# A masked graph layer on one core: PSUM banks redistributed, order constants moved to VectorE, the planned order replaced

## The chip, the cores and the metric

The kernel runs on one core of one Trainium2 chip. The metric is the device time of one execution in microseconds, from several executions of the same program; the median is used. A profile is one further execution, recorded by the hardware profiler. Its span (first to last instruction) is a little shorter than the device time of the same execution.

## The reference

`x` is 4096 x 64, `adj` is 4096 x 4096 (float32, about 67 MB), `weight` is 64 x 64.

```
h = relu(layernorm(x))                        # over the 64 features
support = h @ weight
mask = (adj != 0)
rank = cumsum(mask, axis=1); deg = rank[:, -1:]
k = min(deg, 100)
pos = rank - (deg - k)
w = mask * where(pos > 0, 0.5 ** (k - pos), 0)
out = x + w @ support + bias
```

So each set element of a row of `adj` gets the weight 0.5 to the power of the number of set elements behind it in the row, except that only the last 100 of a row count. The 67 MB of `adj` have to come into the core once; nothing else is large.

## The kernel before, in words

Rows of `adj` are taken in 32 tiles of 128 rows. Two tiles make one unit `u`, two units one group `g` (512 rows), whose sums lie in one PSUM bank. Within a row, the 4096 columns are eight blocks `h` of 512.

The pipeline of one tile `t`, each step one function:

- `load` (L295, on the queue of SyncE): 2 MB from memory into one of four buffers `a_sb` (`NA = 4`). Tiles 0, 1, 28, 29, 30 and 31 are loaded as two halves of 1 MB (`STEP`). The load of tile t needs the buffer of tile t-4, so it waits for that tile's `convert`.
- `convert` (L496, VectorE): float32 to one byte, 64 or 65. One instruction for each load, so of 4096 elements per partition or, where the load is a half, of 2048.
- `flip` (L506, VectorE): 32 x 32 transposes, so that columns of `adj` lie along partitions.
- `totals` (L512, TensorE): counts of set elements by block of 32, into a PSUM bank of pool `t`.
- `split` (L517, ScalarE): reads these counts as bytes into SBUF.
- `suffix` (L526, TensorE): counts behind each block, into a bank of pool `t`.
- `clamp` (L530, VectorE): caps them.
- `place` (L538 and L542, TensorE): the exponent of each element, into four banks of pool `v`, one for each `j`.
- `weigh` (L551, ScalarE): the exponential, four instructions of 1024 elements per partition, each frees one bank of `v`. Tile 31 has three parts of each (`PARTLY`, `PARTED`), 12 instructions.
- `aggregate` (L559, TensorE): weights times `support`; 32 matmuls for each unit, issued in eight pieces of four.

After the last unit of a group come `drain` (L572, ScalarE, adds the bias), `turn_back` (L580, TensorE, transposes), `finish` (L586, VectorE, adds `x`) and, after several groups, `store` (L590, the queue of SyncE). The last group is drained in two pieces (drains 7 and 8, for units 14 and 15).

Ahead of the tiles stands a setup: `fetch` loads `x` (L298), `turn`/`turned` transpose it, `center`, `square`, `relu`, `spread`, `root`, `power`, `support`, `scale` make the layer norm and the product with `weight`, and `first`/`second` split the result `hr` in two halves of its precision (L479 ScalarE, L482 VectorE). Its intermediate data lie in one of the two buffers of weights (`early`, `NW = 2`), so the `weigh` of tile 2, which needs that buffer, waits for all four `second`. Constants for the counting are made on GpSimd: `constants(1)` (L400 to L414, for `place`) and `order_of` (L375 to L389, for `suffix` and `count`).

PSUM has one bank for `t` (`NB = 1`), six for `v` (`NV = 6`) and one for the groups' sums. A buffer of pool `t` takes a whole bank, and totals and suffix of all tiles, and `turn_back`, share the one.

The order of the instructions on every engine is fixed when the program is built. `plan()` holds a list of tasks with a duration, a lag, needs, and a due time from the table `DUE`, plays them forward, and emits them in the order in which they start. `add_manual_dep` at the end keeps each engine in this order. So a change of a number in `DUE` moves instructions, and an engine waits at whatever instruction the order puts next. `warm` fills planned gaps of TensorE with matmuls of zeros (L423).

Of the kernel before, what the change touches and what calls it, by code (L numbers as in the profile page):

```python
# [23 lines left out]
EPS = 1e-5  # L24
# [7 lines left out]
STEP = {t: 4 for t in (0, 1, 28, 29, 30, 31)}  # L32
LOADS = [(t, h, h + STEP.get(t, 8)) for t in TILES for h in range(0, 8, STEP.get(t, 8))]

PARTLY = {31}
PARTED = (0, 1, 0, 2), (1, 2, 0, 1), (1, 2, 1, 2)
DRAINS = [(g, 0, 4, True) for g in range(7)] + [(7, 0, 2, True), (7, 2, 4, True)]
STORES = [(0, 0, 16), (1, 0, 12), (1, 12, 14), (1, 14, 16)]
NA, NM, NT, NW, NV, NB = 4, 4, 4, 2, 6, 1

DUE = {
    "fetch": [-1003, -1847],
    "load": [65, 1148, 1192, 1344, 890, 882, 1059, 807, 177, 1469, 585, 426, -306, 496, -49, 266, 921, 615, 495, 273,
    509, 817, 887, 432, 1250, 832, 1156, 645, 31, 863, 872, 512, 638, 869, 1362, 792, 926, 1009],
    "load_rest": [-481],
    "turn": [-213, 892, -361, 828, -409, -147, 168, -107],
    "turned": [-404, -273, 1152, 128, 503, 511, 433, -263],
    "center": [-857, -641, -1350, -827],
    "square": [139, -1681, -2148, -2029],
    "relu": [217, 890, -64, 143],  # L50
    "spread": [-1274, -1134, -743, -201],
    "support": [458, 166, -823, -732],
    "scale": [31, 1087, -17, 582],
    "root": [-38],
    "power": [-305],
    "constants": [-1199, 288],
    "order_of": [1110],
    "count": [174],
    "counted": [-242],
    "first": [1030, 859, 446, 134],  # L60
    "second": [869, 310, 488, 149],
    "convert": [799, 235, 213, 621, 871, 221, 1137, 339, 665, 170, 840, 839, 269, 846, 1322, 763, 1208, 992, 1053, 1092,
    755, 1566, 506, 1283, 1017, 914, 1881, 1297, 1713, 1456, 1930, 1878, 1817, 1254, 2527, 1603, 1404, 1849],
    "flip": [755, -234, 295, -127, 442, -299, 314, 236, -95, 42, 943, 437, 1189, 848, 1722, 445, 670, 663, 1043, 1071,
    1018, 1159, 1502, 907, 1558, 1730, 1512, 1723, 625, 1907, 1701, 1739, 1719, 1519, 1418, 1515, 1365, 795],
    "totals": [163, 587, 208, 187, -888, 339, 133, -152, 475, 1157, 159, 135, 674, 545, 1071, 817, 439, 1024, 1281,
    1461, 443, 2052, 963, 1181, 926, 1932, 1537, 584, 1513, 1671, 1316, 1615],
    "split": [-294, -174, -1849, -575, -454, -698, -618, -971, -742, -275, 300, 6, -214, 155, -90, -143, 509, 616, 114,
    395, 584, 524, 615, 13, 506, 320, 818, 391, 1992, 1302, 1105, 460],
    "suffix": [265, 470, 626, 553, 76, 351, -120, 701, -560, 193, 222, 311, 159, 444, 810, -221, 772, 1294, 1743, 886,  # L70
    718, 429, 591, 1159, 1296, 2185, 1511, 1501, 2001, 1496, 2127, 1546],
    "clamp": [-739, 475, 354, 317, -585, 294, 102, -276, 538, 118, 920, -398, 130, 1157, 352, 866, 900, 81, -363, 492,
    698, 1569, 702, 757, 515, 1132, 736, 1149, 1495, 1590, 1729, 1541],
    "place": [841, 96, 498, 879, 824, 837, 808, 522, 1103, 1914, 1312, 1548, 862, 1225, 743, 1302, 1785, 1644, 1994,
    1697, 1566, 1560, 1577, 1633, 2537, 1922, 1847, 2364, 2393, 2364, 1714, 1845],
    "weigh": [1655, 1181, 868, 631, 1236, 404, 1584, 1443, 897, 269, 877, 841, 328, 1501, 418, 1096, 1670, 1095, 1290,
    1045, 1295, 1247, 1314, 999, 672, 1559, 1035, 1631, 1070, 1779, 1431, 1276, 2029, 1311, 1734, 1852, 1556, 1640,
    1599, 1881, 1168, 1820, 1423, 545, 1375, 1271, 1659, 2299, 2395, 2281, 2155, 2139, 2062, 2491, 1666, 1651, 1902,
    1875, 1618, 2485, 1751, 1754, 2523, 1796, 2184, 2358, 1409, 2593, 2132, 1541, 1713, 2047, 1583, 1456, 1562, 2282,
    1641, 1846, 1727, 2021, 2924, 2344, 2590, 1925, 1978, 2498, 1946, 1761, 2622, 1817, 2190, 1884, 1953, 2032, 2057,  # L80
    2381, 2020, 2701, 1854, 2394, 2313, 2255, 1976, 2259, 1957, 2012, 1591, 2429, 2382, 2260, 2365, 3172, 2928, 2044,
    3150, 1958, 2643, 2675, 2150, 3338, 2587, 2729, 2343, 2953, 1990, 2517, 2778, 3358, 2745, 2645, 3479, 2076, 3183,
    2758, 2299, 2866],
    "aggregate": [254, 1326, 1623, 59, 522, 1349, 93, 1245, 247, 484, 1268, 1686, 2132, 1190, 2358, 448, 974, 1308,
    1356, 611, 856, 1518, 486, 1545, 1236, 918, 398, 1827, 1513, 1406, 1117, 1500, 1296, 1193, 452, 1811, 1260, 1164,
# [4 lines left out]
    2628, 2119, 2143, 2488, 2511, 1602, 2160, 1962, 2594, 2032, 2291, 2585, 1920, 2821],  # L90
    "drain": [82, 374, 29, 620, 400, 1392, 1843, 1544, 1599],
    "turn_back": [572, 1129, 645, 1544, 2558, 1512, 1987, 1280, 2435],
    "finish": [79, 927, -547, 514, 1225, 592, 1061, 2342, 2532],
    "store": [8458, 8834, 7981, 9977],
}
WAIT = 250, 60, 150, 60, 0
PE, DVE, ACT, POOL, SP = range(5)


def tasks():  # L100
# [534 lines left out]
```

## Time and profile before

| | |
|---|---|
| median of 3 runs | 188.83 us (188.54 to 188.94) |
| the profiled execution: its own time, its span | 188.37 us, 186.7 us |
| TensorE matmul busy (modelled) | 164.9 us, 88% of the span |
| ScalarE busy | 152.1 us, 82% |
| VectorE busy | 146.8 us, 79% |
| GpSimd busy | 18.9 us, 10% |
| moved by DMA | 69.55 MB, mean 373 GB/s over the span |
| `weigh` L551, 136 instructions | 123.2 us, mean 1028 ns |
| `convert` L496, 38 instructions | 84.8 us, mean 2238 ns |
| `aggregate` L559, 512 matmuls | 74.6 us, mean 291 ns |
| `flip` L506, 38 instructions | 40.7 us, mean 1072 ns |
| `split` L517, 32 instructions | 20.3 us, mean 634 ns |
| `clamp` L530, 32 instructions | 15.4 us, mean 481 ns |

The page cuts the span into 40 equal slices of 4.67 us. A digit is the busy share of a slice in tenths. Busy times of single instructions overlap somewhat when they follow each other closely, so four `weigh` of 1081 ns take some 3.7 us, not 4.3. In a timeline each line is a start, a length, an engine, a source line, an operation, its output and input, and how many instructions were merged; in brackets stands the idle time before it and what ended it.

### The profile page before, as it was taken

What the parts mean: (1) busy time and instruction counts of PE and PEld (TensorE: products, weight loads), DVE (VectorE), ACT (ScalarE), POOL (GpSimd) and SP (SyncE); (2) the same over time, 40 slices, a digit from 0 to 9 for tenths busy, and PEclk for the clock granted to TensorE, in tenths of its full rate; (3) what the DMA queues carried; (4) which work ended last, traced back from release to release, by engine and by line L of the source; (5) the groups of instructions that cost most, each with busy time, mean ns of one, the idle gap of its engine ahead of it and who ended that gap; (6) DMA issues with size and microseconds to landing.
All of it is one profiled execution on the core that took longest, in us unless ns stands there. A gap on an engine that the chain in (4) does not pass through costs nothing.

```text
span 186.7 us, 4747 instructions
## 1 busy us (share of the span) xinstructions
PE 164.9 (88%) x2080; PEld 127.3 (68%) x2080; DVE 146.8 (79%) x152; ACT 152.1 (82%) x198; POOL 18.9 (10%) x57
## 2 busy tenths in 40 slices
PE   7999699647989899889998997999898979897982
PEld 5957367435857768667676775877775858685881
DVE  3187499999999997799797899879798989993100
ACT  2773176912999999699999999999969799999951
POOL 7899500000000000000000000000000000000000
PEclk9997569999999999999999999999999999999999
DMA  6999999999999999999999999999999999940020
GB/s 202 390 427 435 435 420 425 416 428 428 428 414 428 434 414 432 428 414 442 411 428 428 418 432 421 418 446 411 428 421 414 413 420 416 417 201 0 12 90 16
DMA packets 6597, 69.55 MB, mean 373 GB/s; under 512 B 944, under 2 KB 1200, under 8 KB 1712
## 3 DMA queue, kind: packets, MB, share of 16 engines
q1 hardware_dynamic: 6416, 69.21, 88.4%
q8 instruction: 16, 0.26, 0.6%
q10 hardware_dynamic: 160, 0.03, 0.1%
q14 instruction: 5, 0.04, 0.1%
HBM read 68.19 MB, written 1.05 MB: 371 GB/s over the span
## 4 chain that ended last, share of the span: by engine, by line
ACT 36%; PE 32%; DVE 15%; POOL 10%; issue 5%; POOLq 0%; ACTq 0%
ACT wk L551 29%; PE acc L559 19%; DVE m L496 7%; ACT sums L517 5%; PE ps L526 5%; PE po L580 3%; DVE mt L506 3%; PE v L542 2%; DVE behind L530 2%; PE v L538 2%; PE tot L512 2%; ACT acc_sb L572 1%; DVE wk L472 1%; DVE hr L482 1%; POOL where L414 1%
## 5 line engine op out<-in xcount | busy, mean ns | idle before, releaser
L551 ACT ACTIVATE wk<-v 128x1024 fp32r<-128x1024 uint8 (+2 forms) x136 | 123.2, 1028 | 2.3 <-PE v L542 2.1
L496 DVE TENSOR_SCALAR m<-a_sb 128x4096 uint8<-128x4096 f32 (+1 forms) x38 | 84.8, 2238 | 5.0 <-DMA a_sb<-in_adj_dram 5.0
L559 PE MATMUL acc<-wk,hr 128*128 128x256 f32 x512 | 74.6, 291 | 3.7 <-ACT wk L551 2.2
L559 PEld LDWEIGHTS acc<-wk,hr 128*128 128x128 f32 x512 | 64.0, 188 | 10.6 <-ACT wk L551 4.3
L506 DVE STREAM_TRANSPOSE mt<-m 128x1024 f32<-128x1024 f32 (+1 forms) x38 | 40.7, 1072 | 0.4
L517 ACT ACTIVATE sums<-tot 128x512 f16<-128x512 uint8 x32 | 20.3, 634 | 16.4 <-PE tot L512 16.4
L530 DVE TENSOR_SCALAR behind<-ps,excess 128x256 f16<-128x256 f32 x32 | 15.4, 481 | 14.1 <-PE ps L526 13.9
L526 PEld LDWEIGHTS <-far 128*128 128x128 f16 x224 | 17.9, 101 | 1.9 <-POOL far L389 1.0
L526 PE MATMUL ps<-sums,far 128*128 128x224 f16 (+6 forms) x224 | 18.5, 225 | 0.7 <-POOL far L389 0.7
L512 PE MATMUL tot<-mt,band 128*32 128x256 f16 x256 | 13.5, 288 | 5.3 <-DVE mt L506 4.3
L538 PE MATMUL v<-behind,where 32*128 32x256 f16 x256 | 13.6, 276 | 2.7 <-DVE behind L530 2.3
L542 PE MATMUL v<-mt,tri 32*32 32x512 f16 x512 | 14.5, 401 | 0.0
L586 DVE TENSOR_TENSOR xr<-po,xr 128x256 f32<-128x256 f32 (+1 forms) x9 | 3.5, 393 | 12.4 <-PE po L580 12.3
L423 PE MATMUL none<-junk 128*128 128x256 bf16 x74 | 11.9, 318 | 1.1 <-DVE junk L307 1.1
L512 PEld LDWEIGHTS <-band 128*32 128x32 f16 x256 | 4.1, 95 | 11.3 <-DVE mt L506 6.1
L423 PEld LDWEIGHTS <-junk 128*128 128x128 bf16 x87 | 8.8, 109 | 3.8 <-DVE junk L307 1.1
L526 PE MATMUL ps<-sums,near 128*128 128x256 f16 x32 | 9.2, 286 | 2.0 <-ACT sums L517 1.8
L572 ACT ACTIVATE acc_sb<-acc,bias_sb 128x512 f32<-128x512 f32 (+1 forms) x9 | 6.1, 679 | 5.4 <-PE acc L559 5.4
L580 PE MATMUL po<-both,acc_sb 128*128 128x64 f32 x64 | 8.7, 275 | 1.9 <-DVE behind L530 1.3
L580 PEld LDWEIGHTS po<-both,acc_sb 128*128 128x128 f32 x64 | 7.8, 191 | 2.8 <-DVE behind L530 1.5
L538 PEld LDWEIGHTS <-where 32*128 32x128 f16 x256 | 4.5, 92 | 7.5 <-issue 4.7
L542 PEld LDWEIGHTS <-tri 32*32 32x32 f16 x512 | 4.4, 88 | 6.9 <-issue 6.9
(86 smaller groups left out, 91.0 us busy)
## 6 DMA issues: line engine op xcount, KB each, us to landing
a_sb<-in_adj_dram SPq DMA_DIRECT2D x26, 2048.0 KB, 15.3
a_sb<-in_adj_dram SPq DMA_DIRECT2D x12, 1024.0 KB, 13.2
xr<-in_x_dram SPq DMA_DIRECT2D x2, 512.0 KB, 3.9
out_dram<-xr SPq DMA_DIRECT2D x1, 512.0 KB, 17.1
out_dram<-xr SPq DMA_DIRECT2D x1, 384.0 KB, 2.3
out_dram<-xr SPq DMA_DIRECT2D x2, 64.0 KB, 1.6
w<-in_L_gnn_weight_dram ACTq DMA_DIRECT2D x2, 16.0 KB, 5.8
bias_sb<-in_L_gnn_bias_dram SPq DMA_DIRECT2D x1, 0.2 KB, 18.8
```

The source lines that it names most:

```text
L423: nc.tensor.matmul(idle[0][:, idle[1]:idle[1] + 2 * P], junk[:, :P], junk, start=not accs, stop=not accs, skip_group_check=True)
L496: nc.vector.tensor_scalar(words[n][:, :(k1 - k0) * P, :].rearrange("p (h q) e -> p h e q", q=P), tiles[t][:, k0 * W:k1 * W].rearrange("p ( ...
L506: nc.vector.transpose(to[:, k0:k1], m_v.rearrange("p (h c l) -> p h c l", c=4, l=SUB))
L512: nc.tensor.matmul(tot[SUB * c:SUB * (c + 1), :V], band[:, SUB - 12 - 4 * a:2 * SUB - 12 - 4 * a], masks[t][:, c, :, a], start=(a == 0), s ...
L517: nc.scalar.activation(sums8[t], pts.pop((t, "n"))[:, :V].bitcast(U8).rearrange("p (i f) -> p f i", f=4)[:, :2, :], AF.Copy, bias=-136.0)
L526: nc.tensor.matmul(o, l, m, start=(k == 0), stop=(k == len(todo) - 1), skip_group_check=True)
L530: nc.vector.tensor_scalar(behind[t], pts.pop((t, "s"))[:, :V], excess, float(MAX_NEIGH), op0=ALU.subtract, op1=ALU.min)
L538: nc.tensor.matmul(vs[t, j][:, a, :], where[q, a, :], behind[t][q, :], start=(a == 0), stop=False, skip_group_check=True)
L542: nc.tensor.matmul(vs[t, j][SUB * c:SUB * (c + 1), :, :], tri[q, q], masks[t][q, c, :, :].rearrange("p i a -> p a i"), start=False, stop=T ...
L551: nc.scalar.activation(wts[u][:, s0:s1, 8 * a0:8 * a1, i, j, :], v[:, s0:s1, 8 * a0:8 * a1], AF.Exp, scale=-LN2, bias=-38.0 * LN2)
L559: nc.tensor.matmul(accs[g][:, at:at + 2 * P], hr[:, h * 4 + 2 * a + s, :, :].rearrange("p s d -> p (s d)"), wts[u][:, s, 8 * a + h].rearra ...
L580: nc.tensor.matmul(pts["o", d][:, k, :], sums[d][:, k * P:(k + 1) * P], both, start=True, stop=True)
```

## The change

- PSUM: pool `t` gets two banks (`NB = 2`), pool `v` five (`NV = 5`).
- `order_of` runs on VectorE instead of GpSimd, ahead of the first tile; `stack` (the constants made from the identity) comes after it. `constants(1)` on GpSimd works on 8 and 32 columns and is broadcast in its last step. The squares get a buffer of their own, so that they no longer share that of the scaled support.
- Tiles 28, 29 and 30 are loaded whole; 0, 1 and 31 in halves (`HALF_LOADS`). Every `convert` is of half a tile, 64 instructions in all. Both halves of a tile that is loaded whole wait for its one load.
- Tile 31 has two parts by column block instead of three, 8 `weigh` instructions; `aggregate` takes its pieces of four matmuls by column block `h` instead of by slot and half.
- Code for units of half a tile (`HALF_UNITS`) and for weights made by VectorE (`QUICK`: `encode`, `take`) is added, with both sets empty: all weights are made by ScalarE, as before.
- The tables `DUE` and `FREE`, and with them the order on all engines. At the end, as built: VectorE has, from tile 30 on, convert 30 twice, clamp 29, flip 30, convert 31 twice, clamp 30, flip 31 twice, finish 6, clamp 31. TensorE has place 30, turn_back 6, totals 31, 12 matmuls of aggregate 14, suffix 31, 8 of aggregate 14, place 31, 12 of aggregate 14, 4 of aggregate 15, turn_back 7, 28 of aggregate 15, turn_back 8. In the kernel before, VectorE has convert 30, flip 30, convert 30, clamp 29, flip 30, convert 31, flip 31, convert 31, clamp 30, flip 31, clamp 31, finish 6, and TensorE has turn_back 6 after place 31, the rest in the same places. ScalarE's order at the end is the same in both, but for the parts of tile 31.

```diff
-STEP = {t: 4 for t in (0, 1, 28, 29, 30, 31)}
-LOADS = [(t, h, h + STEP.get(t, 8)) for t in TILES for h in range(0, 8, STEP.get(t, 8))]
-
-PARTLY = {31}
-PARTED = (0, 1, 0, 2), (1, 2, 0, 1), (1, 2, 1, 2)
+HALF_LOADS = {0, 1, 31}
+HALF_UNITS = set()
...
+LOADS = pieces(HALF_LOADS)
+PIECES = pieces(HALF_LOADS | HALF_UNITS)
+UNITS = pieces(HALF_UNITS)
+
+PARTS = {31: ((0, 4), (4, 8))}
+QUICK = set()
...
-NA, NM, NT, NW, NV, NB = 4, 4, 4, 2, 6, 1
+NA, NM, NT, NW, NV, NB = 4, 4, 4, 2, 5, 2
...
-FREE = 4250, 4450, 5000, 4600, 700
+FREE = 4250, 1300, 3000, 4700, 700
...
-    xt = early[:, 2 * B * D:3 * B * D]
     xs = early[:, :B * D].rearrange("p (b d) -> p b d", d=D)
-    rx = early[:, B * D:2 * B * D].rearrange("p (b i) -> p b i", i=P)
+    xt, sq, rx = (early[:, i * B * D:(i + 1) * B * D] for i in (1, 2, 3))
...
     def order_of():
-        vec = nc.gpsimd
+        vec = nc.vector
...
-            pick, more = (setup.tile([P, 2, P], F32, name=n) for n in ("pick", "more"))
-            idx_v = idx.rearrange("p a j l -> p a (j l)")
+            pick, more = (setup.tile([P, 8], F32, name=n) for n in ("pick", "more"))
+            idx_v = idx.rearrange("p a j -> p (a j)")
...
+    def stack():
+        nc.vector.tensor_add(both, ident[:, :D], ident[:, D:])
+        for h in range(H):
+            q = slice(h * D, (h + 1) * D)
+            nc.vector.tensor_scalar(less[q, h, :], ident[q, q], -1.0 / D, None, op0=ALU.add)
...
+    def half():
+        return ps_t.tile([P, V], F32, tag="t", name="sums")
...
+    def convert(n, i):
+        t, h0, _ = PIECES[n]
+        if i == 0:
+            words[n] = bpool.tile([P, N // E, E], U8, name="m8")
+        h = h0 + 4 * i
+        nc.vector.tensor_scalar(words[n][:, 4 * i * P:4 * (i + 1) * P, :].rearrange("p (h q) e -> p h e q", q=P),
+                                tiles[t][:, h * W:(h + 4) * W].rearrange("p (h e q) -> p h e q", e=E, q=P),
                                 0.0, 64.0, op0=ALU.not_equal, op1=ALU.add)
...
+    def weights(n, part):
+        t, h0, h1 = UNITS[n]
         u, i = t // 2, t % 2
         if u not in wts:
             wts[u] = wpool.tile([P, 2, 16, 2, 4, SUB], F32R, name="wk")
-        a0, a1, s0, s1 = PARTED[part] if t in PARTLY else (0, 2, 0, 2)
-        v = vs[t, j].rearrange("p a i -> p (a i)").bitcast(U8).rearrange("p (x r f) -> p f x r", f=4, r=SUB)
-        nc.scalar.activation(wts[u][:, s0:s1, 8 * a0:8 * a1, i, j, :], v[:, s0:s1, 8 * a0:8 * a1], AF.Exp, scale=-LN2, bias=-38.0 * LN2)
-
-    def aggregate(u, k):
+        x = slice(*(2 * h for h in PARTS.get(n, ((h0, h1),))[part]))
+        return wts[u][:, :, x, i], x
+
+    def weigh(n, j, part=0):
+        to, x = weights(n, part)
+        v = vs[UNITS[n][0], j].rearrange("p h a r -> p (h a r)").bitcast(U8).rearrange("p (x r f) -> p f x r", f=4, r=SUB)
+        nc.scalar.activation(to[:, :, :, j, :], v[:, :2, x], AF.Exp, scale=-LN2, bias=-38.0 * LN2)
...
+    def aggregate(u, h):
         g, at = 2 * u // TG, 2 * u % TG * P
         if g not in accs:
             accs[g] = ps_a.tile([P, W], F32, tag="acc", name="acc")
-        a, s = k // 4, k // 2 % 2
-        for h in range(k % 2 * 4, k % 2 * 4 + 4):
-            nc.tensor.matmul(accs[g][:, at:at + 2 * P], hr[:, h * 4 + 2 * a + s, :, :].rearrange("p s d -> p (s d)"),
-                             wts[u][:, s, 8 * a + h].rearrange("p i j r -> p (i j r)"), start=(k == h == 0),
-                             stop=(k == h == 7), skip_group_check=True)
+        order = order_in(u)
+        for e in range(4):
+            a, s = e // 2, e % 2
+            nc.tensor.matmul(accs[g][:, at:at + 2 * P], hr[:, h * 4 + e, :, :].rearrange("p s d -> p (s d)"),
+                             wts[u][:, s, 2 * h + a].rearrange("p i j r -> p (i j r)"), start=(h == order[0] and e == 0),
+                             stop=(h == order[-1] and e == 3), skip_group_check=True)
```

## The prediction

> **What bounds the kernel now.** I read the slices of the page first, then the times at which loads land, then the timelines of the engines at the end, then the start.
>
> ```profile
> ACT  2773176912999999699999999999969799999951
> DMA  6999999999999999999999999999999999940020
> GB/s 202 390 427 435 435 420 425 416 428 428 428 414 428 434 414 432 428 414 442 411 428 428 418 432 421 418 446 411 428 421 414 413 420 416 417 201 0 12 90 16
> ```
>
> All sixteen DMA engines are busy from slice 1 to 34 at some 425 GB/s. ScalarE is saturated too, but only from slice 10. The issues of the last two loads and, from the query on `a_sb` with the same window, their times to landing:
>
> ```profile
> 149.69 0.80 SPq L295 DMA_DIRECT2D a_sb<-in_adj_dram  x2
> ```
>
> ```profile
> DMA to landing us min/median/max: 14.1/15.2/16.3
> ```
>
> They land at 149.7 + 14.1 = 163.8 and 150.1 + 16.3 = 166.4 us. In the same way tile 5 lands at 37.0, tile 27 at 146.4: 109.4 / 22 = 4.97 us a tile. Tiles 28 to 31, in halves, take (166.4 - 146.4) / 4 = 5.0. So the last row tile is there at 166.4, and 20.3 us of the span follow. VectorE's timeline at the end:
>
> ```profile
> 161.03 1.35 DVE L496 TENSOR_SCALAR m<-a_sb 128x2048 uint8<-128x2048 f32 x1
> ...
> 163.05 1.36 DVE L496 TENSOR_SCALAR m<-a_sb 128x2048 uint8<-128x2048 f32 x1
> ...
> 167.35 1.36 DVE L496 TENSOR_SCALAR m<-a_sb 128x2048 uint8<-128x2048 f32 x1
> 168.60 0.47 DVE L530 TENSOR_SCALAR behind<-ps,excess 128x256 f16<-128x256 f32 x1
> 168.99 0.70 DVE L506 STREAM_TRANSPOSE mt<-m 128x512 f32<-128x512 f32 x1
> ```
>
> The last convert starts 0.95 us after its landing, without a wait: VectorE is a little late. Then TensorE:
>
> ```profile
> 169.12 0.40 PE L538 MATMUL v<-behind,where 32*128 32x256 f16 x8 [0.71 <-DVE behind L530]
> 169.45 0.45 PE L542 MATMUL v<-mt,tri 32*32 32x512 f16 x16
> 169.82 0.41 PE L512 MATMUL tot<-mt,band 128*32 128x256 f16 x8
> 170.80 1.69 PE L559 MATMUL acc<-wk,hr 128*128 128x256 f32 x12 [0.57 <-ACT wk L551]
> ...
> 174.08 0.40 PE L538 MATMUL v<-behind,where 32*128 32x256 f16 x8
> 174.41 0.45 PE L542 MATMUL v<-mt,tri 32*32 32x512 f16 x16
> 174.78 1.10 PE L580 MATMUL po<-both,acc_sb 128*128 128x64 f32 x8
> 175.70 1.66 PE L559 MATMUL acc<-wk,hr 128*128 128x256 f32 x12
> ...
> 178.92 3.56 PE L559 MATMUL acc<-wk,hr 128*128 128x256 f32 x28
> ```
>
> Here is a chain: landing, convert 31, clamp 30, place 30 (169.12), totals 31, aggregate, suffix 31, aggregate, place 31 (174.08), turn_back 6, aggregate, drain 7 (177.46), aggregate, end. ScalarE is beside it, with little reserve. Its start:
>
> ```profile
> 45.46 0.60 ACT L517 ACTIVATE sums<-tot 128x512 f16<-128x512 uint8 x1 [3.44 <-PE tot L512]
> 46.09 7.44 ACT L551 ACTIVATE wk<-v 128x1024 fp32r<-128x1024 uint8 x8
> ```
>
> The weigh of tile 2 could not start before the last `second` (44.79 + 1.26). From there to the end of the block at 177.0 ScalarE does 30 tiles with under 5 us of idleness: 4.2 us a tile, less than the 4.97 of a transfer. It catches up 0.7 us with each tile, so the late start is nearly made good by the end.
>
> [...]
>
> **The change part by part.**
>
> *Order constants.* GpSimd spent 13.58 to 21.62 on these 13 instructions; they vanish there. On VectorE six of one to four columns take about 0.2 each (0.14 to 0.15 busy for such, L395 and L396, plus issue)[...]. They start at about 2.7 and end, with `stack` (0.23 + 0.51), near 6.5. VectorE is idle 3.93 us before its first convert at 9.03, which waits for DMA: hidden, with 2.5 to spare. `center` newly waits for `stack`, and behind it in TensorE stand `spread` and totals 0; it needed the `turned` of 9.88 anyway. Cost 0 on the path. Without that cover it is up to 3 us, at the start.
>
> *The head start.* I add up VectorE's order from the convert at 16.5: convert 1.4, root 0.75, flip 0.7, power 2.0, clamp 0.5, scale 0.7, then converts, scales, flips and `second` of tiles 2 and 3. The last `second` ends near 36 instead of 46. ScalarE begins tile 2 about 8 us sooner, 38 against 46. At 4.2 us a tile it meets the transfers near tile 14, and then waits for them. So these 8 us buy nothing by themselves: they are hidden by the 4.97 us a tile of DMA. This is what the whole first part of the change is worth.
>
> *Converts in halves.* Before, two halves back to back (152.48) reach the next instruction after 2.55; a whole one after 2.5 to 2.7. So 26 more instructions cost 0 to 0.1 each. VectorE needs 2.55 + 1.16 (flip) + 0.40 (clamp) + 0.1 (finish) = 4.2 a tile, 0.7 under the transfers: hidden.
>
> *Two banks for counts and sums.* Totals of the next tile no longer wait for the clamp. VectorE waited 9.1 us, in 13 waits, for suffixes between 46 and 165; that lateness goes, and its backlog before tile 30 with it. What is late next is the landing.
>
> *Whole loads of 28 to 30.* A gain of 0 to 0.3 us by the two rates above, I take 0.2: last landing 166.2, tile 30 at 161.2. The other side: convert 30 now waits for the whole tile, 2.3 us later than its first half landed (158.9). VectorE then runs without a gap from 161.25: +2.55 convert 30, +0.40 clamp 29, +1.16 flip 30, +1.25 convert 31 first half = 166.6, where the second half is there since 166.2. +1.25, clamp 30 +0.47, semaphore: place 30 at 168.4 instead of 169.12.
>
> *Five banks for exponents.* place(t) needs four banks; with one spare instead of two it waits for the third weigh of tile t-1, not the second. Behind it in TensorE stand turn_back, totals and the aggregates, and split 31 waits for these. Clamp 29 ends at 164.3, place 29 takes to 165.1, weigh(29,0) to 166.0, split 30 to 166.5, two weigh at 0.92 to 168.35, place 30 at 168.45. It just ties with VectorE. Price 0 here; if ScalarE is late, all of its lateness up to one weigh, 0.92, at tile 30 and again at 31. I take 168.45, 0.67 sooner than before.
>
> *From place 30 to place 31.* turn_back 6 (0.92) moves ahead of totals 31: place 0.70 + 0.92 + totals 0.34 + twelve matmuls 1.53 + suffix 0.63 + eight matmuls 1.0 = 5.1, against 4.96 before, which held 0.6 of waiting for ScalarE. Flip 31 ends at 169.6, so totals 31 at 170.1 is not held up. Place 31 at 173.55.
>
> *From place 31 to the end.* Without turn_back 6, the twelve matmuls end 2.3 after place 31; now the four weigh of part 0 decide: 0.85 until the first, 0.52 each, so drain 7 starts 2.95 after, before 3.38. The rest of the order is alike: drain, four matmuls, turn_back 7, 28 matmuls (3.4 us), drain 8, turn_back 8, finish, store: 186.7 - 177.46 = 9.24. Part 1 as four weigh of 0.52 instead of eight of 0.28 saves 0.2 beside the matmuls, so nothing. Aggregates by column block: the same 512 matmuls, nothing.
>
> *All weights on ScalarE* is no change: 132 instructions instead of 136, `encode` and `take` are never called.
>
> Sum: 173.55 + 2.95 + 9.24 = 185.74, against 186.7: -0.96 us (0.67 from place 30, -0.14, 0.43). The profiled execution took 188.37 and would take 187.4. The median of the runs, 0.46 higher, becomes 188.83 - 0.96 = **187.9**.
>
> **The rivals.**
>
> *The head start reaches the end*: 46 - 38 = 8 us less, about 181. For it speaks the page's chain (ScalarE 36%) and slices 10 to 37; against it the landing at 166.4. Partial forms (a tail with a better order than I see) give 186 to 187.
>
> *Nothing to be measured*: halves were as fast as wholes (+0.2) and VectorE reaches tile 30 half a microsecond late, because its waits only move. Then place 30 is at 169.1 and only the 0.3 of the end remains: 188.5 to 189.
>
> *Slower by five banks.* If ScalarE's backlog at the end is as before (its weigh(29,2) ended at 169.7), place 30 starts at 169.8 instead of 169.12, and place 31 loses up to 0.92 more in the same way: +0.7 + 0.5 = 190.0. It decides once weigh(29,2) ends after clamp 30. The same wait in all tiles harms only if it takes ScalarE from 4.2 past 4.97 a tile, over 0.75 a tile; below that the transfers hide it. For it: the tie above. Against it: ScalarE has eight microseconds in hand at tile 2.
>
> **How the numbers follow.** Forecast 187.9 (its own range 187.2 to 188.4): 0.50. Head start or better order, below 187.2: 0.08. Nothing to be measured: 0.19. Five banks: 0.23. A measurement of this kernel tells about 0.2% from no change, so faster is below 188.45, slower above 189.2. Faster 0.50 + 0.08 = 0.58, same 0.19, slower 0.23. The range 187.0 to 190.0 goes from the sum with 0.3 more from landing and tail, with some of the better order, to the five banks' price.
>
> **What would show it.** Right: the weigh of tile 2 starts before 40; in the second half ScalarE and VectorE wait, the convert for DMA; the last landing at 166.2; place 30 near 168.4; drain 7 just after the four weigh. Wrong: a landing off by over half a microsecond, DMA slices below 9, place waiting for ScalarE, or a convert that no longer waits for its load at the end.

## The result and the profile after

The changed kernel takes 189.8 us (median of 10 executions, 188.53 to 192.4), the kernel before beside it 188.63 (10, 188.43 to 189.09): ratio 1.0052, 95% interval 1.0027 to 1.0077. The forecast was 187.9. Measured again with 22 executions it is 189.38 against 188.60, ratio 1.0056 (1.0038 to 1.0075). An execution more than 1.5% above the fastest of its kernel counts as slow: the medians in this document are of all executions, the ratios leave the slow ones out.

The profiled execution that came with the result, 192.4 us, had TensorE at half clock for 3.4 us in the tail, so the profile after that is read here is one of the same kernel from an execution of 189.25 us, span 187.27, without such a stretch. Against it stands the profiled execution before: 188.37, span 186.65. The difference to be explained is 0.88 us.

The slices and the last two loads:

```profile
ACT  2864187987999989889999898399999999989840
DMA  5999998999999999999999999999999999931000
GB/s 205 403 430 439 420 432 357 427 427 427 430 430 429 423 430 423 423 434 416 430 427 416 434 427 420 434 427 423 434 416 434 427 418 416 404 140 78 9 14 16
```

```profile
149.40 0.80 SPq L333 DMA_DIRECT2D a_sb<-in_adj_dram  x2
```

```profile
DMA to landing us min/median/max: 14.5/15.5/16.5
```

The transfers are as before: the highest slice has 439 GB/s, before 446, and the last half of tile 31 lands at 149.8 + 16.5 = 166.3, before at 166.4. Whether the data could come sooner no run here tests. ScalarE is at work from slice 5 on, before from 10, and has a hole at slice 25. The head start is there:

```profile
33.81 0.61 ACT L565 ACTIVATE sums<-sums 128x512 f16<-128x512 uint8 x1
34.29 5.71 ACT L613 ACTIVATE wk<-v 128x1024 fp32r<-128x1024 uint8 x6
```

A block of six `weigh` in which tile 2 is begun starts at 34.3; before, the weigh of tile 2 began at 46.1. And the waits of the whole span (engine, tile and line, what it waited for: us in total, times, longest):

```profile
DVE m L539 <- DMA a_sb<-in_adj_dram: 17.0, 23, 3.6
ACT wk L613 <- PE v L599: 12.6, 17, 3.2
```

VectorE now waits for its loads, and ScalarE for exponents that come from them. The tail of VectorE, TensorE and ScalarE, in order of time:

```profile
161.41 2.68 DVE L539 TENSOR_SCALAR m<-a_sb 128x2048 uint8<-128x2048 f32 x2 [0.69 <-DMA a_sb<-in_adj_dram]
...
163.24 1.66 PE L633 MATMUL acc<-wk,hr 128*128 128x256 f32 x12
...
164.83 0.40 PE L595 MATMUL v<-behind,where 32*128 32x256 f16 x8
...
165.53 2.62 DVE L539 TENSOR_SCALAR m<-a_sb 128x2048 uint8<-128x2048 f32 x2
...
165.69 1.02 ACT L613 ACTIVATE wk<-v 128x1024 fp32r<-128x1024 uint8 x1 [0.61 <-PE v L599]
...
167.21 1.94 ACT L613 ACTIVATE wk<-v 128x1024 fp32r<-128x1024 uint8 x2
...
168.17 0.48 DVE L584 TENSOR_SCALAR behind<-sums,excess 128x256 f16<-128x256 f32 x1
...
168.71 0.29 PE L595 MATMUL v<-behind,where 32*128 32x256 f16 x3 [0.58 <-DVE behind L584]
...
169.20 0.37 PE L595 MATMUL v<-behind,where 32*128 32x256 f16 x5 [0.20 <-ACT wk L613]
169.50 0.45 PE L599 MATMUL v<-mt,tri 32*32 32x512 f16 x16
...
169.88 1.10 PE L654 MATMUL sums<-both,acc_sb 128*128 128x64 f32 x8
...
174.86 0.44 PE L599 MATMUL v<-mt,tri 32*32 32x512 f16 x16
...
175.40 2.06 ACT L613 ACTIVATE wk<-v 128x512 fp32r<-128x512 uint8 x4 [0.60 <-PE v L599]
...
177.32 0.50 ACT L646 ACTIVATE acc_sb<-acc,bias_sb 128x256 f32<-128x256 f32 x1
```

Drain 7, before the change:

```profile
177.46 0.47 ACT L572 ACTIVATE acc_sb<-acc,bias_sb 128x256 f32<-128x256 f32 x1 [0.46 <-PE acc L559]
```

Convert 30 waits 0.69 for its whole tile. Place 30 begins at 168.71, earlier than the 169.12 before, but after three of its eight matmuls it waits for ScalarE's third weigh of tile 29 (167.21 + 1.94), which is the price of five banks. Its second half (L599) starts 0.79 after the first, before 0.33: at 169.50, before at 169.45. ScalarE is late here since place 29, the line at 164.83, stood behind twelve matmuls of an aggregate, and the first weigh of tile 29 waited for it until 165.69. Then the end of the program, which the prediction did not price. First before, then after: from the timeline the issue of the last store; from the waits how long SyncE (SP) waited for its landing; from the query on the program's last line SyncE's instructions behind it, with number, durations in ns and first and last start.

```profile
184.12 0.33 SPq L590 DMA_DIRECT2D out_dram<-xr  x1
```

```profile
SPq L630 <- DMA out_dram<-xr: 0.7, 1, 0.7
```

```profile
L630 SPq EVENT_SEMAPHORE  x3: 28/28/28, 184.9 to 185.1; - x3
...
L630 SPq EVENT_SEMAPHORE  x2: 28/28/28, 185.8 to 185.8; - x2
L630 SPq DRAIN  x1: 13/13/13, 185.9 to 185.9; - x1
```

```profile
184.00 0.33 SPq L664 DMA_DIRECT2D out_dram<-xr  x1
```

```profile
SPq L704 <- DMA out_dram<-xr: 1.3, 1, 1.3
```

```profile
L704 SPq EVENT_SEMAPHORE  x5: 28/28/28, 185.6 to 185.9; - x5
...
L704 SPq DRAIN  x1: 120/120/120, 186.4 to 186.4; - x1
```

At the end SyncE waits for the semaphores of all DMAs in five instructions, in a fixed order. The store lands 1.6 us after its issue in both. Before, three of the five waits are done by then, and the drain follows two waits later. After, the first wait already waits for this landing and all five come behind it; then SyncE stands still for 0.41 us more before its drain. From the issue of the last store to the end of the span it is 2.53 us before and 3.27 after.

The 0.88 us along the chain, after minus before, all from these lines:

| stretch | before | after | difference |
|---|---|---|---|
| second half of place 30 starts | 169.45 | 169.50 | +0.05 |
| to the same of place 31 (174.41, 174.86) | 4.96 | 5.36 | +0.40 |
| to drain 7 (177.46, 177.32) | 3.05 | 2.46 | -0.59 |
| to the last store (184.12, 184.00) | 6.66 | 6.68 | +0.02 |
| last store to the end of the span | 2.53 | 3.27 | +0.74 |
| outside the span | 1.72 | 1.98 | +0.26 |

The compute chain ends 0.12 us earlier; 1.00 us is added behind the last store and outside the span.

### The profile page after: what moved, and what is told of

Its sections match the earlier page's. It is cut to its first block, busy times and chain, and to the rows that moved or that the text cites. A ratio compares the mean times of both kernels' runs of the same rounds, so it can differ in the third digit from the quotient of the medians.

```text
span 190.4 us, 4758 instructions
## 1 busy us (share of the span) xinstructions
PE 169.0 (89%) x2081; PEld 131.8 (69%) x2081; DVE 150.2 (79%) x188; ACT 153.3 (80%) x194; POOL 6.8 (4%) x43
## 3 DMA queue, kind: packets, MB, share of 16 engines
HBM read 68.19 MB, written 1.05 MB: 364 GB/s over the span
## 4 chain that ended last, share of the span: by engine, by line
DMA 38%; PE 25%; ACT 18%; DVE 15%; issue 2%; ACTq 0%
DMA a_sb<-in_adj_dram 36%; PE acc L633 15%; ACT wk L613 15%; DVE m L539 10%; PE sums L578 3%; PE v L599 2%; PE sums L654 2%; DVE mt L549 2%; PE v L595 2%; ACT sums L565 2%; DMA xr<-in_x_dram 2%; DVE behind L584 1%; ACT acc_sb L646 1%; DVE hr L520 1%; PE sums L557 1%
## 5 line engine op out<-in xcount | busy, mean ns | idle before, releaser
L613 ACT ACTIVATE wk<-v 128x1024 fp32r<-128x1024 uint8 (+1 forms) x132 | 124.0, 1023 | 13.8 <-PE v L599 13.6
L539 DVE TENSOR_SCALAR m<-a_sb 128x2048 uint8<-128x2048 f32 x64 | 86.0, 1390 | 16.7 <-DMA a_sb<-in_adj_dram 16.6
L565 ACT ACTIVATE sums<-sums 128x512 f16<-128x512 uint8 x32 | 19.8, 620 | 8.1 <-PE sums L557 8.1
L584 DVE TENSOR_SCALAR behind<-sums,excess 128x256 f16<-128x256 f32 x32 | 15.1, 472 | 7.5 <-PE sums L578 7.3
L578 PE MATMUL sums<-sums,far 128*128 128x224 f16 (+6 forms) x224 | 18.3, 223 | 0.0
L557 PE MATMUL sums<-mt,band 128*32 128x256 f16 x256 | 13.5, 289 | 1.3 <-DVE mt L549 1.2
L599 PE MATMUL v<-mt,tri 32*32 32x512 f16 x512 | 14.2, 397 | 0.0
L578 PE MATMUL sums<-sums,near 128*128 128x256 f16 x32 | 9.3, 289 | 1.8 <-ACT sums L565 1.7
L654 PE MATMUL sums<-both,acc_sb 128*128 128x64 f32 x64 | 8.8, 278 | 1.0 <-ACT acc_sb L646 0.6
L654 PEld LDWEIGHTS sums<-both,acc_sb 128*128 128x128 f32 x64 | 7.8, 191 | 2.3 <-ACT acc_sb L646 1.9
L578 PE MATMUL sums<-sums,rest 128*128 128x256 f16 x32 | 9.0, 281 | 0.0
L599 PEld LDWEIGHTS <-tri 32*32 32x32 f16 x512 | 4.4, 87 | 6.6 <-issue 6.6
```

Of the source, the lines that this page charges most:

```text
L539: nc.vector.tensor_scalar(words[n][:, 4 * i * P:4 * (i + 1) * P, :].rearrange("p (h q) e -> p h e q", q=P), tiles[t][:, h * W:(h + 4) * W] ...
L557: nc.tensor.matmul(tot[SUB * c:SUB * (c + 1), r], band[:, SUB - 12 - 4 * a:2 * SUB - 12 - 4 * a], masks[t][:, c, r, a], start=(a == 0), st ...
L565: nc.scalar.activation(sums8[t][:, :, r], pts.pop((n, "n")).bitcast(U8).rearrange("p (i f) -> p f i", f=4)[:, :2, r], AF.Copy, bias=-136.0)
L578: nc.tensor.matmul(o, l, m, start=(k == 0), stop=(k == len(todo) - 1), skip_group_check=True)
L584: nc.vector.tensor_scalar(behind[n][:, r], pts.pop((n, "s"))[:, r], excess, float(MAX_NEIGH), op0=ALU.subtract, op1=ALU.min)
L599: nc.tensor.matmul(vs[t, j][SUB * c:SUB * (c + 1), h0:h1], tri[q, q], masks[t][q, c, r, :].rearrange("p (h r) a -> p h a r", r=SUB), start ...
```

## The experiments

Two theories at first. *Whole loads* (A): convert 30 waits for a whole tile, and this lateness reaches the end. *Turn_back*: its place ahead of totals 31 delays tile 31. After the first four runs the ends of the span were compared, and a third came: *the end of the program* (B), by the number of loads. The semaphores of SyncE's DMAs are taken in turn, eight of them, as the trace names them (101, 103 to 107, 109 and 110, in before as in after): with 38 loads the last store has the one in the fourth closing wait, with 35 or 43 that in the first, with 39 that in the fifth. "Ratio" is against the kernel before on the same chip. "Store to end" and the last store's issue are from each profile; the time less the span is a mean over all its executions (scatter 0.03; for the kernel before it is that of its profile, and its 59 executions beside c1_again have 1.71).

| run | loads | median us | ratio (95%) | last store | store to end | time less span |
|---|---|---|---|---|---|---|
| before | 38 | 188.60 | | 184.12 | 2.53 | 1.72 |
| c1_again | 35 | 189.38 | 1.0056 (1.0038 to 1.0075) | 184.00 | 3.27 | 2.00 |
| e2_halves | 38 | 188.49 | 0.9996 (0.9978 to 1.0013) | 183.67 | 2.55 | 1.99 |
| e3_turn_back | 35 | 189.78 | 1.0045 (1.0025 to 1.0064) | 184.47 | 3.27 | 1.99 |
| e4_gpsimd | 35 | 189.23 | 1.0023 (1.0010 to 1.0036) | 183.85 | 3.29 | 1.95 |
| e5_other_halves | 38 | 188.51 | 0.9998 (0.9981 to 1.0015) | 184.19 | 2.51 | 1.99 |
| e6_halves_43 | 43 | 189.01 | 1.0017 (1.0000 to 1.0033) | 184.04 | 2.70 | 2.00 |
| e7_before_43 | 43 | 188.93 | 1.0018 (1.0009 to 1.0026) | 185.03 | 2.73 | 1.72 |
| e8_tail | 39 | 188.38 | 0.9989 (0.9969 to 1.0009) | 185.03 | 2.42 | 1.98 |
| e9_whole_43 | 43 | 190.42 | 1.0073 (1.0054 to 1.0093) | 184.07 | 2.71 | 1.99 |
| e10_whole_converts | 35 | 189.37 | 1.0025 (1.0008 to 1.0041) | 184.52 | 3.27 | 1.99 |
| e11_two_banks | 38 | 197.67 | 1.0479 (1.0442 to 1.0515) | 194.48 | 2.52 | 1.74 |
| e12_whole_43_later | 43 | 189.39 | 1.0040 (1.0025 to 1.0054) | 184.48 | 2.71 | 1.98 |
| e13_before_vector | 38 | 188.73 | 1.0000 (0.9982 to 1.0018) | 184.63 | 2.54 | 1.99 |

**c1_again**: the changed kernel, no edit.

> The changed kernel once more, for a second profile and time. Theory A (the landing of tile 30, loaded whole, and the order behind it set the end): about 189.5 us; tile 30 lands near 162.5, the last half near 167, place 31 near 175 to 176 if TensorE's clock stays at full speed in the tail. Rival B (a drop of TensorE's granted clock in the tail makes the loss): the drop from 172 to 176 us is there again, and without it the time is below 188.8.

The loss is there again: +0.78 us in the medians, 1.05 by the ratio. The drop of the clock in the tail is not there, and the time is 189.25 all the same, so rival B falls. But tile 30 landed at 161.4, the last half at 166.3, and place 31 began at 174.5: theory A had them all later.

**e2_halves**: 28 to 30 in halves.

```diff
-        nc.sync.dma_start(tiles[t][:, k0 * W:k1 * W], adj_v[:, t // HT, t % HT, k0 * W:k1 * W])
+        step = 4 if t in (28, 29, 30) else k1 - k0
+        for c in range(k0, k1, step):
+            nc.sync.dma_start(tiles[t][:, c * W:(c + step) * W], adj_v[:, t // HT, t % HT, c * W:(c + step) * W])
```

> The changed kernel with tiles 28, 29 and 30 loaded as two halves again, all orders kept. Theory A: convert 30 starts 2.3 us sooner, near 160.3, clamp 29, place 29, weigh 29, split 30 and place 30 follow 1 to 1.5 us sooner, so the time is 188.3 to 188.8 against 189.5. Rival B (clock) and rival C (five banks make place wait for ScalarE): within 0.2 us of the changed kernel.

The whole loss goes. In its tail convert 30 no longer waits, and place 30 comes earlier, but by 0.27 us and not by 1 to 1.5, since clamp 30 now waits for TensorE's suffix:

```profile
167.90 0.48 DVE L586 TENSOR_SCALAR behind<-sums,excess 128x256 f16<-128x256 f32 x1 [0.31 <-PE sums L580]
...
168.93 0.37 PE L597 MATMUL v<-behind,where 32*128 32x256 f16 x5 [0.20 <-ACT wk L615]
```

But only 0.33 us of the profiles' difference to c1_again lies in the chain (last store 184.00 to 183.67); 0.72 lies behind the last store. The edit had changed two things, where the tiles are cut and how many loads there are.

**e3_turn_back**: turn_back 6 and finish 6 behind place 31.

```diff
+    late = [x for x in steps if x[2:] in (("turn_back", (6,)), ("finish", (6,)))]
+    steps = [x for x in steps if x not in late]
+    at = [x[2:] for x in steps].index(("place", (31,))) + 1
+    steps[at:at] = late
```

> The changed kernel with turn_back 6 and finish 6 put behind place 31, as in the kernel before. Theory A: totals 31 and place 31 come 1.0 us sooner, drain 7 then waits for the twelve matmuls of aggregate 14 (0.4 us given back): 0.5 us less than the changed kernel, about 189.0. If the landing of the last half or ScalarE decides instead, nothing changes; if the move was right, 0.4 us more.

In this run the second store goes out ahead of finish 6, so the rows of group 6 leave without their sums. The second halves of place 30 and 31, and drain 7:

```profile
170.04 0.45 PE L599 MATMUL v<-mt,tri 32*32 32x512 f16 x16
...
174.83 0.44 PE L599 MATMUL v<-mt,tri 32*32 32x512 f16 x16
...
177.82 0.47 ACT L646 ACTIVATE acc_sb<-acc,bias_sb 128x256 f32<-128x256 f32 x1 [0.39 <-PE acc L633]
```

From place 30 to place 31 it takes 4.79 us, in c1_again 5.36: 0.57 gained. From there to drain 7 it takes 2.99 instead of 2.46, since drain 7 now waits for the twelve matmuls behind turn_back 6: 0.53 given back, so the theory of a net gain falls. That drain 7 is 0.50 later than in c1_again is another matter: place 30 is 0.54 later already, ahead of anything that the edit moves, and the last half of tile 31 lands 0.78 later (167.05 against 166.27).

**e4_gpsimd**: `vec = nc.gpsimd` in `order_of` again, in the changed kernel.

> The changed kernel with the order constants made by GpSimd again, in its first place: the setup is later by some 3.5 to 4 us, since count stands ahead of center on TensorE. Theory A (the head start at the beginning is hidden by the transfers): within 0.2 us of the changed kernel. Rival D (the head start reaches the end): 3 us more or above.

Not slower than c1_again: 0.15 us faster in the median, and 0.6 by the ratio, whose interval lies below that of c1_again. No profile here explains the 0.6; c1_again has six of its 22 executions above 190 us, this run two. The edit is a weak test of the head start. It was to make the setup 3.5 to 4 us later, but the block of six `weigh` in which tile 2 is begun starts at 35.60 instead of 34.29, 1.3 us later, and the kernel before has its tile 2 at 46.1. What is hidden by the transfers is this 1.3.

**e5_other_halves**: as e2, but `t in (10, 11, 12)`; 28 to 30 stay whole.

> The changed kernel with tiles 10 to 12 loaded in two halves each and tiles 28 to 30 whole as they were: 38 loads as before the change, all orders kept. Theory A (the loss comes from the whole loads of 28 to 30): as the changed kernel, 189.4 us. Theory B (the loss is mostly at the end of the program: SyncE's closing waits for the DMA semaphores come in a fixed order; with 35 loads the last store's semaphore is in the first of five, and the others run only after the landing; with 38 it is in the fourth): last finish to end of span 2.55 us instead of 3.3, time 188.6 to 188.8; what remains over the halves of 28 to 30 (188.5) is the whole loads' own price, 0.1 to 0.3.

Theory A falls: the loss goes just as well with the halves far from the tail (ratio 0.9998, e2_halves 0.9996). The last store is issued 0.19 us later than in c1_again, and the end is 0.76 shorter.

**e6_halves_43**: as e2, and 10 to 14 in halves too.

> Halves for 28 to 30 as in the earlier run that took the loss away, and halves for 10 to 14 too: 43 loads, so that the last store is back on the semaphore of 35 loads (eight in rotation). Theory A: as with halves for 28 to 30 alone, 188.5 us. Theory B: 0.65 us longer, 189.1 to 189.2, with 3.2 to 3.3 us from the last finish to the end of the span.

Half a microsecond slower than e2_halves, with the store back in the first wait; of it the end accounts for 0.15 only, and theory B had forecast 0.65.

**e7_before_43**: the kernel before, tiles 10 to 14 in halves, the same three lines.

> The kernel before with one edit: tiles 10 to 14 loaded in halves, 43 loads instead of 38, nothing else changed. Theory A: 188.6 us, no change. Theory B: 0.65 us longer, 189.2 to 189.3; last finish to end 3.2 to 3.3 us against 2.6.

The end grows in the kernel before too, by 0.20, and the time by 0.34 (0.17 to 0.49) by the ratio: the mechanism is no property of the changed kernel. But the expected 0.65 was too much: SyncE's pause of 0.41 us does not lie behind the landing here. So the 0.74 are two things: three more waits behind the landing (all five instead of the last two), 0.2, and a pause, 0.41, with a slower drain behind it, 0.54 together.

**e8_tail**: e2's halves, one more load (tile 14), and steps moved in the order.

```diff
+    move(("suffix", (31,)), ("split", (31,)))
+    move(("aggregate", (14, 2)), ("suffix", (31,)))
+    move(("place", (31,)), ("clamp", (31,)))
+    move(("drain", (7,)), ("weigh", (31, 3, 1)))
+    move(("turn_back", (7,)), ("drain", (8,)))
+    move(("finish", (7,)), ("turn_back", (7,)))
+    move(("store", (2,)), ("finish", (7,)))
```

> The changed kernel with halves for 28 to 30 and for 14 (39 loads: last store's semaphore in the fifth closing wait), and in the tail: suffix 31 straight after split 31 with one aggregate fewer ahead of it, place 31 straight after clamp 31, drain 7 behind the second weights of 31, its turn_back, finish and store behind drain 8. Theory B with TensorE's and ScalarE's waits as read from the trace (0.55 us of ScalarE ahead of weigh 31, 1.0 us of TensorE ahead of the first aggregate of 15, 0.45 of turn_back 7 on the way): 187.0 to 187.6 us. If the end of the tail is set by something else (the last landing, say): 188.4.

No gain that can be told from none, and no run here is clearly faster than the kernel before. From place 30 to the last store it takes 15.29 us, in e2_halves 15.23: ScalarE loses its wait ahead of weigh 31, but TensorE now waits 0.69 for drain 7 behind all eight weigh. A wait moved.

**e9_whole_43**: 28 to 30 whole, `t in range(5, 13)` in halves.

> The changed kernel with tiles 5 to 12 in halves and 28 to 30 whole: 43 loads, so that the last store's semaphore is again in the first closing wait, as with 35 loads, but SyncE's queue holds 8 more instructions. In the changed kernel SyncE pauses 0.41 us between the fifth closing wait and the next instruction, after the landing; in the kernels with 38 and 43 loads a pause of that length lies ahead of the landing or is not there. If the pause hangs on how many instructions SyncE has run: last store's issue to end 2.70 us instead of 3.27, time 0.55 us under the changed kernel, 188.8; if it comes with that semaphore or with the whole loads: 3.27 and 189.4.

The pause is not tied to the semaphore: with the same one the end is 2.71, and no pause stands before the drain.

```profile
SPq L706 <- DMA out_dram<-xr: 1.3, 1, 1.3
```

```profile
L706 SPq EVENT_SEMAPHORE  x6: 17/28/28, 185.7 to 186.2; - x6
L706 SPq DRAIN  x2: 7/10/13, 186.0 to 186.1; - x2
```

The profiled execution took 188.76, as expected, but the median is 190.42: a miss, and the largest open point.

**e14_whole_43_look**, the same kernel once more, and **e12_whole_43_later**, `t in range(10, 18)`:

> The same kernel as the run with tiles 5 to 12 in halves and 28 to 30 whole, for a second profile: its first profiled execution took 188.76 us, while most timed ones took 190 to 191. If most executions of it lose in one place (a granted clock under 0.97 at one stage), a profile near 190.4 shows that place; if the profile is near 188.8 again, the place stays open.

> The changed kernel with tiles 10 to 17 in halves (not 5 to 12) and 28 to 30 whole: 43 loads again. If the end of the program decides (2.70 us from the last store's issue with 43 loads, 3.27 with 35, 2.53 with 38): 188.7 to 188.9. If it was not the number of loads but something that halves early in the stream do to the work behind them, which the run with tiles 5 to 12 (190.42) would be an instance of: 189.4 or more.

Two executions of e14: 188.95, and the profiled one, 192.55. TensorE's granted clock in the slices, first e9, then e14:

```profile
PEclk9998599999999999999999996999999999999999
```

```profile
PEclk9997599999999999999999975999999999997999
```

Same program: in e14 the clock is halved for 6.8 us near 112 and for 3.4 us near 173 us, in e9 for 3.4 us near 112 and not in the tail. The last store is 3.79 us later (187.86 against 184.07), and it comes in two pieces. Between the second halves of place 30 and place 31 lie 6.92 us instead of 5.31: the twelve matmuls of aggregate 14, which fall into the half-clock stretch, take 2.85 instead of 1.63, and the suffixes behind them are slower too (measured in the profile that came with the result, half clock from 172.96 to 176.37: from the suffixes' start to the next aggregate 1.04 us, in c1_again 0.63). That is 1.61 us for the stretch in the tail. The other 2.17 are there when the second half of place 30 starts (171.81 against 169.64), and the last load has landed 1.50 later (167.85 against 166.35). This lateness of the loads grows at loads that land near 35, 78 and 163 us and not near 112, so the stretch there is not seen to cost anything. That the longer executions of e9 lose in the same way is not shown: six of its 19 have a mean granted clock of 0.972 or 0.973, as the profiled one, and took from 188.36 to 191.38 us.

e12 gave 189.39 where 188.7 to 188.9 was expected. Its end is 2.71 as forecast, but its last store is 0.48 later than in c1_again: tile 28 comes 0.7 us late, the last half of tile 31 lands at 167.05 instead of 166.27, and the last store follows 17.43 us behind it, in c1_again 17.73. In this profile the transfers take back what the end gives. Whether halves early in the stream cause such a late load stays open; c1_again and e3_turn_back have one too, with 6.5 us between two landings instead of 4.9.

**e10_whole_converts**: one convert for a whole tile again.

```diff
-        h = h0 + 4 * i
+        size = 4 if n in (0, 1, 2, 3, len(PIECES) - 2, len(PIECES) - 1) else 8
+        if i * 4 % size:
+            return
```

> The changed kernel with the converts of the 28 middle tiles, and of 28 to 30, in one instruction per tile, as before the change, instead of two halves (30 instructions of VectorE fewer); all else kept. Forecast of the prediction: halves cost nothing at the end, so 189.4 as the changed kernel. The time less the span is 1.99 us in every kernel built on the changed one and 1.72 in the two built on the one before: if VectorE's number of instructions sets it, it falls by 0.2 or more here; else it stays at 1.99.

189.37 against 189.38: halves cost nothing in the median, as forecast. By the ratio (1.0025 against 1.0056, the intervals just meet) a cost of some 0.6 us is not excluded. VectorE's number of instructions does not set what lies outside the span (1.99 us here, 2.00 in c1_again).

**e11_two_banks**: the kernel before with `bufs=2` for pool `t` and `bufs=5` for `v`.

> The kernel before with one edit: two buffers for counts and sums and five for exponents, its own order kept. If VectorE's and ScalarE's waits at those banks reached the end of the kernel: TensorE's totals and sums come earlier, 187.9 or less; if the fifth bank costs at the end (place waits for the weights of two tiles back): 189 to 190; if both are hidden by the transfers: 188.6. The time less the span says whether the banks set it: 1.99 or 1.72.

9 us slower. Its waits between 20 and 170 us:

```profile
ACT sums L517 <- PE tot L512: 22.1, 14, 6.7
DVE behind L530 <- PE ps L526: 19.2, 19, 2.2
...
PE v L538 <- ACT wk L551: 7.6, 14, 1.1
```

Place waits for a weigh 14 times, 7.6 us in all, and totals and suffixes stand behind it in TensorE's order; ScalarE and VectorE wait for those. In the same window place waits 0.4 us in 2 times in the kernel before and 1.4 in 4 in c1_again. So these five and two banks are cheap in the order made for them and dear in the old one. The waits point to the fifth bank of `v`; the second bank of `t` was changed together with it. (One bank for `t` under the changed order was not tried: that order takes the second bank before the first is free.)

**e13_before_vector**: the kernel before, `vec = nc.vector` in `order_of`.

> The kernel before with one edit: the order constants (order_of) on VectorE instead of GpSimd, its own order kept. The head start is hidden by the transfers: 188.6 us, and the weights of the first tiles 5 us or more earlier. If the constants' engine sets what lies outside the span, the time less the span rises from 1.72 toward 1.99 us; the run with the constants of the changed kernel back on GpSimd took 0.04 of it away, so 1.76 at most is expected.

No change in the time, but a wide scatter, 187.08 to 190.62. The weights of tiles 0 to 2 come 1.4 to 2.0 us earlier, not 5 or more (tile 2 at 44.73, before at 46.09), so this run too tests little of the head start. The time less the span goes from 1.72 to 1.99, which was not expected: this edit alone brings the 0.27 us. Yet undone in the changed kernel (e4) it gives back 0.04. So it is one way to get them, not the only one, and why stays open.

## Why the prediction was wrong

**Right.** Order constants hidden ahead of the first convert (the profile that came with the result has them from 2.19 to 5.27 us, the seven instructions of 128 columns with 0.23 to 0.34 each, `stack` to 5.71, and VectorE then idle for 3.50 us; the forecast end, 6.5, was an estimate, as no such instruction had been measured on VectorE), convert halves at nothing in the median (e10_whole_converts), VectorE and ScalarE waiting for data, the last landing (166.3; forecast 166.2), drain 7 set by the four weigh (2.8 us after place 31; forecast 2.95), and the stretch from drain 7 to the last store as before (+0.02). That the whole head start bought nothing fits the profiles: tile 2 is begun some ten microseconds sooner, and the last landing and the second half of place 30 are where they were. The runs test only the 1.3 us of it that e4_gpsimd takes away.

In the profiled execution -0.96 us was forecast and +0.88 measured, 1.84 apart: 0.74 behind the last store, 0.72 at place 30, 0.26 from there to place 31, 0.26 outside the span, 0.02 from drain 7 to the last store, less 0.16 from place 31 to drain 7.

**The step that failed and made the loss** is "The rest of the order is alike: drain, four matmuls, turn_back 7, 28 matmuls (3.4 us), drain 8, turn_back 8, finish, store: 186.7 - 177.46 = 9.24". It is 187.27 - 177.32 = 9.95. The order is alike, down to the store; what follows the store is not. I costed the whole loads as transfers and as a wait of convert 30, and not as three DMAs fewer, which put the last store's semaphore in another closing wait and SyncE's pause behind the landing: +0.74. That the number of loads does it, and not where they are whole, is shown by e5_other_halves. The profiles agree: from the last store to the end it is 3.27 to 3.29 us in all with 35 loads, 2.51 to 2.55 in all with 38, and 2.70 to 2.73 in all with 43. So do the times of the kernels built on the changed one: the ratios with 35 loads are 1.0023 to 1.0056, every interval above 1, those with 38 or 39 are 0.9989 to 0.9998, every interval around 1. The share of the waits alone is shown by e7_before_43 (0.20); that the pause comes with 35 loads and not with that semaphore, by e9_whole_43. Two runs do not fit in their times: with 43 loads, e9_whole_43 and e12_whole_43_later have the shorter end and are no faster than c1_again. For e12 the profile shows the late load, for e9 the cause is open.

Where the pause falls can be counted in the traces: in all ten profiles that show it, it stands behind SyncE's 79th recorded instruction. With 35 loads (84 instructions in all) this is the fifth closing wait; in e5_other_halves (87) it is the second; in the other kernels with 38 loads (89) it is the last store, so that the landing covers the pause; with 43 loads (92 or 94) it comes before the end. What makes SyncE pause is not shown. On the DMA queue q14, which the page labels "instruction", a packet of 8 KB starts 0.6 us after the pause in c1_again (at 187.0) and in before (at 185.5, the pause there ahead of the first closing wait), and no profile with 43 loads has such a packet in its last ten microseconds, or a pause at its end.

**A second omission**: "The profiled execution took 188.37 and would take 187.4" took what lies outside the span for the same. It is 0.26 us more.

**The gain that did not come.** The step is "It just ties with VectorE. Price 0 here". The sum had -0.67 at place 30; its second half is measured at +0.05. Of the 0.72 between, 0.26 is the start (168.71 for 168.45: the tile came at 161.4 for 161.2, convert 30 ended at 164.09 for 163.8). The other 0.46 is the tie: weigh(29,2) ended at 169.15 and not at 168.35, as place 29 stood behind twelve matmuls that the prediction left out, and place 30 stopped 0.20 us in its middle. This is read from the trace; no run takes it away. From place 30 to place 31 I had +0.14; it is +0.40, as turn_back 6 takes 1.03 on the way, not 0.92, and the eight matmuls ahead of place 31 take 1.12, not 1.0. With -0.59 (forecast -0.43) from place 31 to drain 7, the chain gains 0.12 and not 0.96.

**The rivals.** "Slower by five banks" had the sign, and its wait is there: with 0.46 us it takes away most of the gain forecast at place 30. It does not make the loss, since e2_halves has the same wait of 0.20 us and loses nothing. "Nothing to be measured" had the chain right; what came behind the last store and outside the span carried it over the 189 us at which that rival ended.

## What to carry to other kernels

When a change alters how many DMAs a queue issues, look behind the last one: which closing wait holds its semaphore, and what the queue still has to run after the landing, a pause included. Compare the last landing, the last store, the span and the total time separately before you explain a small difference by the compute chain: in twelve of the sixteen profiles the last store comes 17.4 to 18.1 us behind the last landing, and that landing is anywhere from 165.8 to 167.2. An edit that takes effect in two ways at once (where loads are cut, and how many there are) needs a control that does only one of them. And read from the trace how far an edit did what it was made for: e4_gpsimd and e13_before_vector moved the start by 1.3 and 1.4 us, where some four and five were expected.

## What the runs showed of the hardware

SyncE's five closing waits start 0.06 to 0.09 us apart once their semaphores are there (0.064 and 0.085 in before, 0.070 to 0.075 in after), so that a last store in the last of them (39 loads: 2.42 us from store to end) instead of the first (43 loads: 2.70) saves 0.28. In the ten profiles that show its pause, SyncE pauses for 0.4 us behind its 79th recorded instruction (0.46 us idle in before, 0.43 in after, between other closing waits 0.04 to 0.06), so the place in the program moves with the number of instructions ahead: it is ahead of the first closing wait in before, between the second and the third in e5_other_halves, behind the fifth in c1_again.

In the middle of the stream whole tiles land 4.9 us apart, but single ones come 0.6 to 1.6 us later than that; in 13 of the 16 profiles one that lands between 106 and 113 us does (before at 112.06, 6.35 us behind the one ahead of it; after at 108.73, 6.46 behind). Why is open.

In the traces of before and after TensorE's granted clock is recorded as 1.0 or 0.5 and as nothing between. Half-clock stretches that end before the program does last 10.24 us in before, 6.83, 3.41 and 3.41 in after, and they start whole multiples of 3.41 us apart (in e14 at 16.67, 112.24 and 173.68: 28 and 18 of them; in after at 15.95, 114.93 and 172.96: 29 and 17). In the kernel before, the profile has one such stretch, 16 to 26 us; five profiles of the changed kernel and of those built on it (after, e8_tail, e9_whole_43, e12_whole_43_later, e14_whole_43_look) have another in the slice from 112 to 117 us, and two (after and e14) have one near 173 us. What brings these stretches about no run here tests.
